# LayerNorm moved from the data into the weights of a float32 q/k projection, with deeper prefetch of x and of the mixing's rows

## The chip, the cores and the metric

The kernel runs on one core of one Trainium2 chip. A core has TensorE (PE in the profile, with its weight loads as PEld), VectorE (DVE), ScalarE (ACT), GpSimd (POOL) and SyncE (SP), which here issues every DMA. The engines run their own instruction lists in order and meet at semaphores. The metric is the device time of one execution in microseconds (us).

## The reference

Two gated residual steps on x of shape (8, 512, 2048), all float32. `_layernorm` normalises over the last axis (2048) without weights.

```python
x = x + tanh(g_xattn[0]) * xattn(_layernorm(x), ctx, mask, Wq, bq, Wk, bk, Wv, bv, Wo, bo)
x = x + tanh(g_ffn[0])   * ffn(_layernorm(x), W_res, W_pre, W_post, ...)

# xattn: patches of 128 along the last axis, 8 heads of 32
q = Wq @ qp + bq;  k = Wk @ qp + bk;  val = Wv @ vp + bv      # Wq, Wk, Wv: 256 x 512; qp from layernorm(x), vp from ctx
attn = softmax(where(mask, q^T k / sqrt(32), -1e9));  o = gelu(attn @ val)
out = (Wo @ o + bo) * mask

# ffn: 4 streams of 512 in each row of 2048
x_norm = x * rsqrt(mean(x*x) + eps)
H_res = sinkhorn_log(x_norm @ W_res.T + base, 50 iterations)   # 4 x 4 for each row
H_pre, H_post = softmax(x_norm @ W_pre.T + ..), softmax(x_norm @ W_post.T + ..)
y = (sum_n H_pre[n] * stream[n]) @ W_branch
out stream i = sum_j H_res[i, j] * stream[j] + H_post[i] * y
```

The normalised row d of x is (x[d] - mean[d]) * rstd[d]. In the projection d is the contracted index, so rstd[d] and mean[d] belong to the partition on which row d lies.

## The kernel before

The work is cut into 32 blocks (8 batches of 4), each 512 columns of x, with 4 steps of 128 columns. For block n, `load_x` brings four tiles of 128x512 into the pool `xp` (16 tiles). `proj(n)` makes q and k. For each of the four tiles, GpSimd writes the normalised xn (L500), ScalarE rounds it to a float16 xh (L505), GpSimd makes the float16 rest xl (L507). Then for each of four 128-row groups m of q and k TensorE adds twelve float16 matmuls in PSUM: WqkH on xh, WqkH on xl, WqkL on xh for each of four tiles (L518 to L520). ScalarE and VectorE evacuate the sum as a float16 pair ev (L522, L523), which goes to DRAM (qd) and comes back as QS and KS (`stack`, L535).

After that, for each step: `smax` (L569, L571), `expo` (L595, L597), `vproj` (L559, a float32 matmul), `attv` (L612 to L620); for each block `outp` (mask L632, gl L657, output projection L667 to L670, the sum into the x tile L671, and its store to x1s, L674). An x tile is taken at the load and given back after the store in `outp`, one block after its attention. `stats(b)` reads x and xT of the next batch for its mean, rstd and logits (`finish_stats` gives rstd and nb = -mean * rstd).

When a batch is through, `ffn` runs its Sinkhorn chain on VectorE (L840 to L863), and the rows are mixed: 20 groups of 128 rows by `mixv` (ScalarE, GpSimd and VectorE: xpre L920 to L925, y on TensorE L905 to L907, w L939 to L949), and 12 groups by `mixp` on TensorE, at the end of the program (L959 to L1004). `mixv` loads its four rows-tiles x1 from x1s as it starts (pool of 4) and writes through w (2 tiles).

The order is set by hand in the main loop, by the string ORDER and by priorities; the framework then places each engine's instructions by a modelled timeline, so a change of one operation can move others. `load_x` stands at letter "l":

```python
if LXP == 4 and p == 3 and n > 0 and n + 3 < NTOT:
    defer(D_LX, "lx", lambda n=n: load_x(n + 3))
```

D_LX and D_OUT are 0, so these are issued at once.

Of the kernel before, what the change touches and what calls it, by code (L numbers as in the profile page):

```python
# [19 lines left out]
P = 128  # L20
# [5 lines left out]
BLK = 512  # L26
NBLK = S // BLK
# [8 lines left out]
CT_ACT = False  # L36
MH_ACT = False
XS_ACT = False
LXP = 4
POOLMIX = lambda i, j: j == 1 and i > 0  # L40
BUF_GP = 1
BUF_OP = 1
BUF_XHP = 5
BUF_XNP = 2
BUF_XTP = 4
BUF_CTP = 2
BUF_QDP = 3
# [9 lines left out]
MIXL = 1  # L57
HALF = 1
ORDER = "MeoaMgPlsMMvSMpOM"
BUF_W = 2  # L60
BUF_X1 = 4
BUF_PJ = 1
BUF_PH = 1
BUF_EP = 2
BUF_XPRE = 1
PSTEPS = (0,1,1,2)
SP0 = 1
XH_POOL = lambda c: False
CAP = 1.0
NORM0 = True  # L70
D_MH = 0
# [1 line left out]
D_X1 = 0  # L73
D_OUT = 0
D_ST = 0
D_LX = 0
CT_PRE = False
BUF_XP = 16
PE_MIX = ((), (), (), (), (3,), (0, 1, 2, 3), (0, 1, 2, 3), (1, 2, 3))
SPLITS = (1, 1, 1, 1, 1, 1, 1, 1)  # L80
CHAINS = ((0,), (1,), (2,), (3,), (4,), (5,), (6,), (7,))
# [1 line left out]
PE_IN = ((), (), (), (), (), (), (), ())  # L83
# [16 lines left out]
def gated_xattn_mhc_kernel(  # L100
# [22 lines left out]
    B = x.shape[0]  # L123
    NTOT = B * NBLK
# [4 lines left out]
    def ctile(shape, dt, name):  # L129
        return const.tile(shape, dt, tag=name, name=name)  # L130
# [13 lines left out]
    onesb = ctile([P, P], F32, "onesb")  # L144
    V.memset(onesb, 1.0)

    WqkH = ctile([P, 4, 512], F16, "WqkH")
    WqkL = ctile([P, 4, 512], F16, "WqkL")
    Wv = ctile([P, 4, DK], F32, "Wv")
    WoH = ctile([P, 2, 512], F32R, "WoH")  # L150
    WoL = ctile([P, 2, 512], F32R, "WoL")
# [22 lines left out]
    mrow_d = dram.tile([6, B * S], BF16, tag="mrow_d", name="mrow_d")  # L174
    mneg_d = dram.tile([1, B * S], F16, tag="mneg_d", name="mneg_d")
    brow_d = dram.tile([3, 512], F32, tag="brow_d", name="brow_d")


    QS = [ctile([99, NH, SB], F16, f"QS{i}") for i in range(NS)]
# [6 lines left out]
    xnp = ctx.enter_context(tc.tile_pool(name="xnp", bufs=BUF_XNP))  # L186
# [32 lines left out]
    rawx = {}  # L219
    nmean = {}  # L220
    rstd1 = {}
    nb1 = {}
    sq2 = {}
    x1s = {}
    G4 = {}
# [24 lines left out]

    def finish_stats(b, nm, var):
        r = rsqrt(ln0, var, eps_ln, 4, "ln1")
        nb = ln0.tile([P, 4], F32, tag="nb1", name="nb1")
        V.tensor_tensor(nb, nm, r, ALU.mult)
        nmean[b], rstd1[b], nb1[b] = nm, r, nb

    with tc.tile_pool(name="set", bufs=1) as st:

# [66 lines left out]
        for t in range(2):  # L325
            sl = slice(256 * t, 256 * t + 256)
            V.tensor_scalar(wq[:, :, sl], wq[:, :, sl], al[:, t : t + 1], None, ALU.mult)
        A.copy(WqkH, wq)
        V.tensor_tensor(WqkL, wq, WqkH, ALU.subtract)
        for t in range(2):  # L330
            V.tensor_scalar(bqs[:, 2 * t : 2 * t + 2], bcol[:, 2 * t : 2 * t + 2], al[:, t : t + 1], None, ALU.mult)

# [10 lines left out]
        var0 = stile([P, 4], F32, "var0")  # L343
        V.tensor_copy(var0, mv[:, :, 1])
        finish_stats(0, nm, var0)


        mh = stile([B * 16, 3, P], BF16, "mh")
# [91 lines left out]
    def stats(b):  # L440

        lgs = xsp.tile([P, 512], F32, tag="lgs", name="lgs", bufs=1)
        for q4 in range(5):
            if q4 > 0:
                flush(lambda e: e[2] == "st")
                lg = ps_t.tile([P, 512], F32, tag="t", name="lgx")
                for g in range(4):
                    T.matmul(lg[32 * g : 32 * g + 32, :], Wm[:, 4 * q4 - 4 + g, :], xts[g], start=True, stop=True)  # L448
                if q4 == 1:
                    V.tensor_copy(lgs, lg)  # L450
                else:
                    V.tensor_tensor(lgs, lg, lgs, ALU.add)
            if q4 < 4:
                xts = []

                def ld(q4=q4, xts=xts):
                    for g in range(4):
                        xt_ = xtp.tile([P, 512], F32, tag="xTt", name="xTt")
                        k = 4 * q4 + g
                        SY.dma_start(xt_, xT[b, k * P : (k + 1) * P, :])  # L460
                        xts.append(xt_)

                defer(D_ST, "st", ld)
# [12 lines left out]
        sq = lnp.tile([P, 4, NBLK], F32, tag="sq1", name="sq1")  # L476
        for c in range(4):
            for k in range(NBLK):
                xs = xtp.tile([P, BLK], F32, tag="xTt", name="xs")
                (A if XS_ACT else SY).dma_start(xs, x[b, c * P : (c + 1) * P, k * BLK : (k + 1) * BLK])  # L480
                A.activation(xs, xs, AF.Square, bias=nm[:, c : c + 1], accum_out=sq[:, c, k : k + 1])
            if c % 2:
                yield 1
        var = lnp.tile([P, 4], F32, tag="var1", name="var1")
        V.tensor_reduce(var, sq, AX.X, ALU.add)
        V.tensor_scalar(var, var, 1.0 / S, None, ALU.mult)
        finish_stats(b, nm, var)
        yield 1

    qds = {}  # L490

    def proj(n):

        b, k = divmod(n, NBLK)
        flush(lambda e: e[2] == "lx")
        xt = xtile[n]
        hs, ls = [], []
        for c in range(4):
            xn = xnp.tile([P, BLK], F32, tag="xn", name="xn")
            G.tensor_scalar(xn, xt[c], rstd1[b][:, c : c + 1], nb1[b][:, c : c + 1], ALU.mult, ALU.add)  # L500
            h = xhp.tile([P, BLK], F16, tag="xh", name="xh")
            if XH_POOL(c):
                G.tensor_copy(h, xn)
            else:
                A.copy(h, xn)  # L505
            l = xhp.tile([P, BLK], F16, tag="xl", name="xl")
            G.tensor_tensor(l, xn, h, ALU.subtract)  # L507
            hs.append(h)
            ls.append(l)
        if NORM0:  # L510
            yield
        qd = qdp.tile([2, 4, 2, P, BLK], F16, tag="qd", name="qd")
        qds[n] = qd
        for m in range(4):
            ps = ps_p.tile([P, BLK], F32, tag="p", name="qk")
            ms = slice(m * P, (m + 1) * P)
            for c in range(4):
                T.matmul(ps, WqkH[:, c, ms], hs[c], start=(c == 0), stop=False)  # L518
                T.matmul(ps, WqkH[:, c, ms], ls[c], start=False, stop=False)  # L519
                T.matmul(ps, WqkL[:, c, ms], hs[c], start=False, stop=(c == 3))  # L520
            ev = evp.tile([P, 2, BLK], F16, tag="ev", name="ev")
            A.activation(ev[:, 0, :], ps, AF.Identity, bias=bqs[:, m : m + 1])  # L522
            V.scalar_tensor_tensor(ev[:, 1, :], ps, bqs[:, m : m + 1], ev[:, 0, :], ALU.add, ALU.subtract)  # L523
            defer(D_QD, "qd", lambda m=m, ev=ev: SY.dma_start(qd[m // 2, 0:2, m % 2].rearrange("t p s -> p t s"), ev))
            yield

    def stack(m):
# [362 lines left out]

    def mix(b, maps):
        E, cst, pre, prc, post, rec, HR = maps
        for c in range(4):
            if c in PE_IN[b - B]:
                yield from mixp(b, c, maps, True)
            elif c not in PE_MIX[b - B]:
                yield from mixv(b, c, maps)

    def branch(pt, ph, pl, y):

# [8 lines left out]
    def mixv(b, n, maps):  # L909

        E, cst, pre, prc, post, rec, HR = maps
        x1 = []
        for j in range(4):
            t = fp.tile([P, 512], F32, tag="x1", name="x1", bufs=BUF_X1)
            SY.dma_start(t, x1s[b][n * P : (n + 1) * P, 512 * j : 512 * j + 512])
            x1.append(t)
# [20 lines left out]
        for i in range(4):  # L937
# [12 lines left out]
            defer(D_OUT if live[0] else 0, "out", lambda i=i, w=w: SY.dma_start(out[b, n * P : (n + 1) * P, 512 * i : 512 * i + 512], w))  # L950
            yield 1

    def mixp(b, n, maps, inp=False):
# [56 lines left out]
    def run(gen, steps=None):  # L1010
        for _ in gen:
            pass

    run(proj(0))
    stack(0)
    vproj(0)
    for t in range(2):
# [29 lines left out]
    def act(c, t):  # L1047
# [18 lines left out]
            if p == 2:  # L1066
                at("stack", stack, NSB * (n + 1) + 1)
        elif c == "l" and live_:
            if LXP == 4 and p == 3 and n > 0 and n + 3 < NTOT:
                defer(D_LX, "lx", lambda n=n: load_x(n + 3))  # L1070
            if LXP == 5 and p == 2 and n > 0 and n + 3 < NTOT:
                defer(D_LX, "lx", lambda n=n: load_x(n + 3))
            if p == LXP and n > 1 and n + 2 < NTOT:
                defer(D_LX, "lx", lambda n=n: load_x(n + 2))
# [121 lines left out]
```

## Time and profile before

| | |
|---|---|
| median of 3 runs | 1835.11 us (1830.48 to 1844.21) |
| the profiled execution | 1828.05 us, span 1825.9 us |
| TensorE busy | 1547.1 us (85%) |
| VectorE busy | 1382.3 us (76%) |
| ScalarE busy | 1069.4 us (59%) |
| GpSimd busy | 602.8 us (33%) |
| mean granted TensorE clock | 0.932 |
| DMA | 330.60 MB, mean 181 GB/s |

The profile is of one execution. Busy time is the union of an engine's instructions; "L518" is line 518 of the kernel before. A group line gives engine, operation, output and inputs, shape and count, then busy time, mean time of one, and the idle time ahead of it with what ended it. A wait line reads: engine and line, what it waited for, then total us, number of waits, longest. Matmuls are pipelined, so their own durations overlap, and the distance between two starts tells what one costs. Each float32 matmul appears as two instructions.

### The profile page before, as it was taken

To read this page: it belongs to the slowest core of one execution; us is meant where nothing else is said; L and a number is where in the kernel's file an instruction comes from. 1 tells how busy PE (TensorE), PEld (TensorE's weight loads), DVE (VectorE), ACT (ScalarE), POOL (GpSimd) and SP (SyncE) were. 2 spreads that over 40 slices of the span, in tenths; PEclk is the share of its full clock that TensorE was granted. 3 is DMA by queue.
4 is the path that set the end of the run, shared out by engine and by line. 5 is a ranking of instruction groups with operands and counts; after the bars stand their busy time and mean duration, and the time that the engine had idled before them with its cause. 6 is when DMAs were issued, how large, how long until landed. Compare 5 with 4: busy or idle time off the path is not lost.

```text
span 1825.9 us, 32268 instructions
## 1 busy us (share of the span) xinstructions
PE 1547.1 (85%) x10517; PEld 901.0 (49%) x10517; DVE 1382.3 (76%) x4201; ACT 1069.4 (59%) x2030; POOL 602.8 (33%) x511
## 2 busy tenths in 40 slices
PE   3998999989889888889878888799888889768887
PEld 2554555555555554545544445455455555543333
DVE  7434345877888778888888879889898998998761
ACT  2386466646555656558565475566665566755454
POOL 0512222322232243342444333444334442321121
PEclk7999999999999988999988999899999999989999
DMA  6478696467646855568555784468755565523443
GB/s 214 139 209 256 208 258 194 140 174 232 180 134 200 254 169 165 151 192 269 162 154 164 214 251 144 139 196 259 215 154 165 148 189 147 172 93 119 144 157 117
DMA packets 353237, 330.60 MB, mean 181 GB/s; under 512 B 53351, under 2 KB 251303, under 8 KB 353070
## 3 DMA queue, kind: packets, MB, share of 16 engines
q1 hardware_dynamic: 353070, 328.55, 60.6%
q8 instruction: 83, 1.36, 0.3%
q14 instruction: 84, 0.69, 0.1%
HBM read 226.71 MB, written 101.16 MB: 180 GB/s over the span
## 4 chain that ended last, share of the span: by engine, by line
PE 37%; DVE 23%; DMA 18%; issue 9%; ACT 9%; POOL 4%; SPq 1%; ACTq 0%; POOLq 0%; DVEq 0%
PE vp L559 5%; DVE w L946 4%; DMA xs<-in_x_dram 4%; PE qk L518 3%; PE qk L519 3%; DMA out_dram<-w 3%; PE qk L520 3%; DMA x<-x1s 2%; PE mx L1000 2%; DMA x1s<-xt 2%; PE lgx L448 2%; DVE mx L571 2%; PE op L667 2%; DVE W L844 2%; PE mx L1001 2%
## 5 line engine op out<-in xcount | busy, mean ns | idle before, releaser
L559 PE MATMUL vp<-Wv,ct 128*128 128x256 f32 x1024 | 272.4, 418 | 16.7 <-DMA ct<-in_cx_dram 15.1
L500 POOL TENSOR_SCALAR xn<-xt,ln_r,nb 128x512 f32<-128x512 f32 x128 | 105.5, 826 | 501.2 <-DMA xt<-in_x_dram 385.7
L559 PEld LDWEIGHTS vp<-Wv,ct 128*128 128x128 f32 x1024 | 207.4, 210 | 68.0 <-issue 18.6
L518 PE MATMUL qk<-xh,WqkH 128*128 128x512 f16 x512 | 199.2, 390 | 29.4 <-ACT xh L505 16.3
L946 DVE SCALAR_TENSOR_TENSOR w<-x,Et,w 128x512 f32<-128x512 f32 x180 | 180.0, 1001 | 49.6 <-POOL w L944 34.0
L519 PE MATMUL qk<-xl,WqkH 128*128 128x512 f16 x512 | 197.9, 387 | 4.3 <-POOL xl L507 4.0
L520 PE MATMUL qk<-xh,WqkL 128*128 128x512 f16 x512 | 197.6, 386 | 0.0
L571 DVE TENSOR_REDUCE mx<-smax 128x8 f32<-128x1024 f32 x128 | 154.9, 1210 | 41.7 <-PE smax L569 41.3
L507 POOL TENSOR_TENSOR xl<-xn,xh 128x512 f16<-128x512 f32 x128 | 156.3, 1228 | 76.0 <-ACT xh L505 70.4
L597 ACT ACTIVATE e<-sT,ebi,esc 128x1024 f32<-128x1024 f32 x128 | 153.4, 1198 | 18.0 <-PE sT L595 17.9
L523 DVE SCALAR_TENSOR_TENSOR ev<-qk,bqs,ev 128x512 f16<-128x512 f32 x128 | 94.5, 739 | 77.5 <-ACT ev L522 76.1
L667 PE MATMUL op<-gh,WoH 128*128 128x512 f32 x256 | 120.9, 474 | 35.3 <-DVE ev L523 31.1
L944 POOL TENSOR_TENSOR w<-w,pj 128x512 f32<-128x512 f32 x60 | 80.1, 1334 | 213.1 <-ACT w L939 113.7
L505 ACT CAST xh<-xn 128x512 f16<-128x512 f32 x128 | 78.3, 612 | 103.7 <-POOL xn L500 102.9
L522 ACT ACTIVATE ev<-qk,bqs 128x512 f16<-128x512 f32 x128 | 86.9, 679 | 85.0 <-PE qk L520 78.7
L673 ACT ACTIVATE junk<-xt,nmean 128x512 bf16<-128x512 f32 x128 | 91.6, 716 | 73.9 <-DVE xt L671 41.3
L850 DVE TENSOR_TENSOR W<-E,uv 128x64 f32<-128x64 f32 x392 | 119.4, 307 | 5.4
L844 DVE TENSOR_TENSOR W<-E,uv 128x64 f32<-128x64 f32 x352 | 117.1, 335 | 4.8
L612 PE MATMUL u<-e,onesb 128*32 128x256 f32 x1024 | 102.7, 403 | 10.5 <-DVE mq L573 3.8
L668 PE MATMUL op<-gl,WoH 128*128 128x512 f32 x256 | 107.1, 418 | 0.0
L669 PE MATMUL op<-gh,WoL 128*128 128x512 f32 x256 | 106.6, 417 | 0.0
L632 POOL TENSOR_TENSOR o<-o,mb 128x1024 f32<-128x1024 f32 x32 | 75.6, 2364 | 93.2 <-ACT o L627 85.9
(287 smaller groups left out, 3504.6 us busy)
## 6 DMA issues: line engine op xcount, KB each, us to landing
xt<-in_x_dram SPq DMA_DIRECT2D x128, 256.0 KB
ct<-in_cx_dram SPq DMA_DIRECT2D x128, 256.0 KB
xTt<-in_xT_dram SPq DMA_DIRECT2D x128, 256.0 KB
qd<-ev SPq DMA_DIRECT2D x128, 256.0 KB
x1s<-xt SPq DMA_DIRECT2D x128, 256.0 KB
xs<-in_x_dram SPq DMA_DIRECT2D x112, 256.0 KB
QS<-qd SPq DMA_DIRECT2D x192, 128.0 KB
KS<-qd SPq DMA_DIRECT2D x192, 128.0 KB
```

Source lines behind the costliest of these rows:

```text
L507: G.tensor_tensor(l, xn, h, ALU.subtract)
L518: T.matmul(ps, WqkH[:, c, ms], hs[c], start=(c == 0), stop=False)
L519: T.matmul(ps, WqkH[:, c, ms], ls[c], start=False, stop=False)
L520: T.matmul(ps, WqkL[:, c, ms], hs[c], start=False, stop=(c == 3))
L559: T.matmul(ps[:, h, :], ct[:, c, :], Wv[:, c, :], start=(c == 0), stop=(c == 3))
L571: V.tensor_reduce(mx, sc, AX.X, ALU.max)
L597: A.activation(e32, sc, AF.Exp, bias=ebi[:, t : t + 1], scale=esc[:, t : t + 1])
L667: T.matmul(ps, WoH[:, e, cs], gh[:, e], start=(e == 0), stop=False)
L668: T.matmul(ps, WoH[:, e, cs], gl[:, e], start=False, stop=False)
L844: V.tensor_tensor(W4[:, h], E4[:, h], vb[:, h], ALU.mult)
L850: V.tensor_tensor(W4[:, h], E4[:, h], ub[:, h], ALU.mult)
L946: V.scalar_tensor_tensor(w, x1[j], E[:, n, 4 * j + i : 4 * j + i + 1], w, ALU.mult, ALU.add)
```

## The change

The projections of q and k no longer read a normalised copy of x. With w = W * rstd per contracted row, W @ ((x - mean) * rstd) = w @ x - w @ mean. So `weights(b, m)` makes, for each batch b and group m, a float32 tile of scaled weights (GpSimd, four instructions of 128x128), multiplies it with the negated mean on TensorE (four matmuls with one column), and VectorE adds the bias. The scaled Wq and Wk are kept in DRAM (wqk_d) and loaded anew for each batch after the first. `proj` then has four float32 matmuls per group on the x tiles themselves; xn, xh, xl, WqkH and WqkL are gone. For the next batch, groups 0 and 1 are prepared at the end of `stats`, groups 2 and 3 in the last block of the batch that is running, into a pool of 6 tiles.

The x pool has 20 tiles, and `load_x` runs four blocks ahead. In `mix`, the four x1 tiles of the next 128 rows are loaded after the second of four output tiles of the present ones (`fetch`, 8 tiles), and w has 3 tiles. The pool of xh and xl, now used by `mixp` alone for the halves of its branch, has 1 tile of each (5 before).

```diff
-LXP = 4
-BUF_XHP = 5
-BUF_XNP = 2
+BUF_XHP = 1
+BUF_WQ = 6
-BUF_W = 2
-BUF_X1 = 4
+BUF_W = 3
+BUF_X1 = 8
-BUF_XP = 16
+BUF_XP = 20
...
+    def weights(b, m, src=None):
+        w = wqp.tile([P, 4, P], F32, tag="wq", name="wqb")
+        if src is None:
+            SY.dma_start(w, wqk_d[m])
+            src = w
+        for c in range(4):
+            G.tensor_scalar(w[:, c], src[:, c], rstd1[b][:, c : c + 1], None, ALU.mult)
+        bp = ps_t.tile([P, BLK], F32, tag="t", name="bp")[:, 0:1]
+        for c in range(4):
+            T.matmul(bp, w[:, c], nmean[b][:, c : c + 1], start=(c == 0), stop=(c == 3))
+        bi = ln0.tile([P, 1], F32, tag=f"bi{m}", name="bi")
+        V.tensor_tensor(bi, bp, bqs[:, m : m + 1], ALU.add)
+        wqb[b, m] = (w, bi)
...
-        A.copy(WqkH, wq)
-        V.tensor_tensor(WqkL, wq, WqkH, ALU.subtract)
+        for m in range(4):
+            SY.dma_start(wqk_d[m], wq[:, :, m * P : (m + 1) * P])
...
+        for m in range(4):
+            weights(0, m, wq[:, :, m * P : (m + 1) * P])
...
         finish_stats(b, nm, var)
+        for m in range(2):
+            weights(b, m)
...
-        for c in range(4):
-            xn = xnp.tile([P, BLK], F32, tag="xn", name="xn")
-            G.tensor_scalar(xn, xt[c], rstd1[b][:, c : c + 1], nb1[b][:, c : c + 1], ALU.mult, ALU.add)
-            h = xhp.tile([P, BLK], F16, tag="xh", name="xh")
...
-            l = xhp.tile([P, BLK], F16, tag="xl", name="xl")
-            G.tensor_tensor(l, xn, h, ALU.subtract)
...
+            if (b, m) not in wqb:
+                weights(b, m)
+            w, bi = wqb[b, m]
             for c in range(4):
-                T.matmul(ps, WqkH[:, c, ms], hs[c], start=(c == 0), stop=False)
-                T.matmul(ps, WqkH[:, c, ms], ls[c], start=False, stop=False)
-                T.matmul(ps, WqkL[:, c, ms], hs[c], start=False, stop=(c == 3))
+                T.matmul(ps, w[:, c], xt[c], start=(c == 0), stop=(c == 3))
...
+            if k == NBLK - 1 and m < 2 and (b + 1, 1) in wqb:
+                weights(b + 1, m + 2)
...
+        own = [c for c in range(4) if c not in PE_IN[b - B] and c not in PE_MIX[b - B]]
+        ahead = {}
+
+        def fetch(c):
+            if c in ahead or c not in own:
+                return
+            ahead[c] = []
+            for j in range(4):
+                t = fp.tile([P, 512], F32, tag="x1", name="x1", bufs=BUF_X1)
+                SY.dma_start(t, x1s[b][c * P : (c + 1) * P, 512 * j : 512 * j + 512])
+                ahead[c].append(t)
...
+            elif c in own:
+                fetch(c)
+                yield from mixv(b, c, maps, ahead[c], lambda c=c: fetch(c + 1))
...
+            if i == 1:
+                after_first()
...
     run(proj(0))
+    load_x(NBLK)
...
-            if LXP == 4 and p == 3 and n > 0 and n + 3 < NTOT:
-                defer(D_LX, "lx", lambda n=n: load_x(n + 3))
...
+            if p == 3 and n > 0 and n + 4 < NTOT:
+                load_x(n + 4)
```

More of the change, by code (lines that the diff above doesn't have):

```diff
@@ L67 @@
 SP0 = 1
-XH_POOL = lambda c: False
 CAP = 1.0
@@ L75 @@
 D_ST = 0
-D_LX = 0
 CT_PRE = False
-BUF_XP = 16
+BUF_XP = 20
 PE_MIX = ((), (), (), (), (3,), (0, 1, 2, 3), (0, 1, 2, 3), (1, 2, 3))
@@ L145, in gated_xattn_mhc_kernel @@
     V.memset(onesb, 1.0)
-    WqkH = ctile([P, 4, 512], F16, "WqkH")
-    WqkL = ctile([P, 4, 512], F16, "WqkL")
     Wv = ctile([P, 4, DK], F32, "Wv")
@@ L176, in gated_xattn_mhc_kernel @@
     brow_d = dram.tile([3, 512], F32, tag="brow_d", name="brow_d")
+    wqk_d = dram.tile([4, P, 4, P], F32, tag="wqk_d", name="wqk_d")
     QS = [ctile([99, NH, SB], F16, f"QS{i}") for i in range(NS)]
@@ L185, in gated_xattn_mhc_kernel @@
     xsp = ctx.enter_context(tc.tile_pool(name="xsp", bufs=2))
-    xnp = ctx.enter_context(tc.tile_pool(name="xnp", bufs=BUF_XNP))
+    wqp = ctx.enter_context(tc.tile_pool(name="wqp", bufs=BUF_WQ))
     xhp = ctx.enter_context(tc.tile_pool(name="xhp", bufs=BUF_XHP))
@@ L221, in gated_xattn_mhc_kernel @@
     rstd1 = {}
-    nb1 = {}
+    wqb = {}
     sq2 = {}
@@ L252, in finish_stats @@
         r = rsqrt(ln0, var, eps_ln, 4, "ln1")
-        nb = ln0.tile([P, 4], F32, tag="nb1", name="nb1")
-        V.tensor_tensor(nb, nm, r, ALU.mult)
-        nmean[b], rstd1[b], nb1[b] = nm, r, nb
+        nmean[b], rstd1[b] = nm, r
+    def weights(b, m, src=None):
[11 more added lines that the diff above has]
+        wqb[b, m] = (w, bi)
     with tc.tile_pool(name="set", bufs=1) as st:
@@ L494, in proj @@
         b, k = divmod(n, NBLK)
-        flush(lambda e: e[2] == "lx")
         xt = xtile[n]
-        hs, ls = [], []
-        for c in range(4):
-            xn = xnp.tile([P, BLK], F32, tag="xn", name="xn")
-            G.tensor_scalar(xn, xt[c], rstd1[b][:, c : c + 1], nb1[b][:, c : c + 1], ALU.mult, ALU.add)
-            h = xhp.tile([P, BLK], F16, tag="xh", name="xh")
[L502 to L505, printed above, removed]
-            l = xhp.tile([P, BLK], F16, tag="xl", name="xl")
-            G.tensor_tensor(l, xn, h, ALU.subtract)
-            hs.append(h)
-            ls.append(l)
         if NORM0:
@@ L515, in proj @@
             ps = ps_p.tile([P, BLK], F32, tag="p", name="qk")
-            ms = slice(m * P, (m + 1) * P)
+            if (b, m) not in wqb:
+                weights(b, m)
+            w, bi = wqb[b, m]
             for c in range(4):
-                T.matmul(ps, WqkH[:, c, ms], hs[c], start=(c == 0), stop=False)
-                T.matmul(ps, WqkH[:, c, ms], ls[c], start=False, stop=False)
-                T.matmul(ps, WqkL[:, c, ms], hs[c], start=False, stop=(c == 3))
+                T.matmul(ps, w[:, c], xt[c], start=(c == 0), stop=(c == 3))
             ev = evp.tile([P, 2, BLK], F16, tag="ev", name="ev")
-            A.activation(ev[:, 0, :], ps, AF.Identity, bias=bqs[:, m : m + 1])
-            V.scalar_tensor_tensor(ev[:, 1, :], ps, bqs[:, m : m + 1], ev[:, 0, :], ALU.add, ALU.subtract)
+            A.activation(ev[:, 0, :], ps, AF.Identity, bias=bi)
+            V.scalar_tensor_tensor(ev[:, 1, :], ps, bi, ev[:, 0, :], ALU.add, ALU.subtract)
             defer(D_QD, "qd", lambda m=m, ev=ev: SY.dma_start(qd[m // 2, 0:2, m % 2].rearrange("t p s -> p t s"), ev))
+            if k == NBLK - 1 and m < 2 and (b + 1, 1) in wqb:
+                weights(b + 1, m + 2)
             yield
@@ L895, in mix @@
                 yield from mixp(b, c, maps, True)
-            elif c not in PE_MIX[b - B]:
-                yield from mixv(b, c, maps)
+            elif c in own:
+                fetch(c)
+                yield from mixv(b, c, maps, ahead[c], lambda c=c: fetch(c + 1))
     def branch(pt, ph, pl, y):
@@ L907, in branch, with mixv @@
             T.matmul(y, pl[:, e, :], WbH[:, e, :], start=False, stop=(e == 3))
-    def mixv(b, n, maps):
+    def mixv(b, n, maps, x1, after_first):
         E, cst, pre, prc, post, rec, HR = maps
[L912 to L916, printed above, removed]
         for _ in range(MIXL):
@@ L949, in mixv @@
             V.scalar_tensor_tensor(w, y, post[:, n, i : i + 1], w, ALU.mult, ALU.add)
-            defer(D_OUT if live[0] else 0, "out", lambda i=i, w=w: SY.dma_start(out[b, n * P : (n + 1) * P, 512 * i : 512 * i + 512], w))
+            SY.dma_start(out[b, n * P : (n + 1) * P, 512 * i : 512 * i + 512], w)
+            if i == 1:
+                after_first()
             yield 1
@@ L1068, in act @@
         elif c == "l" and live_:
-            if LXP == 4 and p == 3 and n > 0 and n + 3 < NTOT:
-                defer(D_LX, "lx", lambda n=n: load_x(n + 3))
[L1071 to L1074, printed above, removed]
+            if p == 3 and n > 0 and n + 4 < NTOT:
+                load_x(n + 4)
         elif c == "s" and live_ and t + AHEAD < NT_:
```

## The prediction

> **What bounds the kernel now.** I first cut the span into four stages (busy time per engine in given stretches; the columns are length, then busy us and instruction count of PE, PEld, DVE, ACT, POOL, then granted clock, DMA share, GB/s).
>
> ```profile
> 0.00:60.00 60.00, 24.57 (x76) 14.14 (x77) 40.67 (x93) 16.68 (x22) 14.92 (x19) 0.72 0.55 174
> 60.00:600.00 540.00, 497.11 (x3739) 298.08 (x3738) 335.04 (x948) 318.92 (x618) 157.31 (x139) 0.97 0.68 199
> 600.00:1560.00 960.00, 807.73 (x5735) 491.83 (x5733) 818.46 (x2359) 594.84 (x1143) 378.45 (x306) 0.92 0.63 186
> 1560.00:1826.00 266.00, 217.67 (x970) 96.97 (x970) 188.16 (x803) 138.92 (x249) 52.16 (x48) 0.95 0.40 131
> ```
>
> The reader is to see two regimes. From 60 to 600 us (attention, no mixing yet) TensorE is busy 92% at clock 0.97 and VectorE 62%: TensorE bounds. From 600 to 1560 us, with the mixing, both stand at 84 to 85% and the clock is 0.92: no engine is full, they wait for each other. The last 266 us hold no projection (the next view shows x0). The same query for line 518 alone, the first of the three f16 matmuls, says where the change acts:
>
> ```profile
> 60.00:600.00 540.00, 81.25 (x214) 20.73 (x213) 0.97 0.68 199
> 600.00:1560.00 960.00, 112.74 (x288) 28.48 (x288) 0.92 0.63 186
> 1560.00:1826.00 266.00, 0.00 (x0) 0.00 (x0) 0.95 0.40 131
> ```
>
> Next, TensorE's timeline, since mean durations overlap: the starts count.
>
> ```profile
> 76.50 0.38 PE L518 MATMUL qk<-xh,WqkH 128*128 128x512 f16 x1
> 76.72 0.38 PE L519 MATMUL qk<-xl,WqkH 128*128 128x512 f16 x1
> 76.94 0.38 PE L520 MATMUL qk<-xh,WqkL 128*128 128x512 f16 x1
> ...
> 1751.59 1.02 PE L1000 MATMUL mx<-ys,QD 128*128 128x512 f32 x2
> 1752.45 1.02 PE L1001 MATMUL mx<-xc,HD 128*128 128x512 f32 x2
> ```
>
> One f16 matmul of 512 columns takes 0.216 us from start to start, one float32 matmul of that size (two instructions) 0.86 us. Last, the waits from 600 to 1560 us:
>
> ```profile
> POOL xn L500 <- DMA xt<-in_x_dram: 191.0, 54, 15.8
> ACT w L939 <- DMA out_dram<-w: 42.4, 31, 5.4
> ACT pj L924 <- DMA x<-x1s: 37.5, 24, 3.9
> PE op L667 <- DVE ev L523: 26.0, 18, 4.9
> ACT xpre L920 <- DMA x<-x1s: 18.9, 15, 3.9
> ```
>
> ScalarE stands for 98.8 us behind the mixing's transfers; POOL's 191 us are spare time, since TensorE waited for xh and xl only some 20 us in the whole span.
>
> **The projections.** Three f16 matmuls (0.648 us) become one float32 matmul (0.86 us): +0.212 us for each of 512. By the view of L518: 214 x 0.212 = 45 us in the early stage, 288 x 0.212 = 61 us in the middle, 2 us before.
>
> **The bias products.** 32 groups of four float32 matmuls with one column. The nearest row is rawp L467 (128x32, float32), whose instructions follow each other every 112 ns, two to a matmul: 0.22 us each, 0.9 us a group, 28 us in all. Four groups fall in setup, about 9 us in the early stage, 16 us in the middle. Ends: 0.14 us each, as L420 (128x1) ran (18 us), or 0.44, as L406 ran at half clock (56 us).
> They can also wait: 28 groups need a fresh weight tile. The SP queue issues its load once the old tile is released, POOL scales it, then TensorE may go. Behind a bias product stands all of TensorE's queue, first of all the output projection and the next q/k columns; behind the load, every transfer, as all are issued by SP. In the changed order 12 of the 28 groups have only 78 to 160 entries of TensorE's list (some 240 a block, so a third to two thirds of a block, 15 us or more) between the release and the product; for the others it is over 370 or nothing is released. A 256 KB load has taken 4 to 5 us in the chain of waits, the four scalings 1 us. Ends: 0, and 12 x 5 = 60 us if no distance is left; I take 5 us, because of the distance.
>
> **What goes from POOL, ScalarE and VectorE.** POOL loses xn (105.5 us) and xl (156.3 us), ScalarE the cast (78.3 us). POOL gains 128 scalings of 128x128: L500 takes 826 ns for four times as much, so from 207 ns each up to 826; I take 250, 32 us. VectorE's 32 bias additions (129 ns, as kap L323) are 4 us, against 3 us for the old nb. POOL sets no end here, but it slows VectorE. Read instruction by instruction, w L946 (two SBUF inputs) takes 740 ns (median of 81) where no POOL instruction overlaps it, and 1218 ns (mean of 99) where one does; the reduction L571 takes 1215 ns either way. Adding such excesses by the overlapping POOL line gives 54.7 us for L507 (74 cases) and 8.2 us for L500 (26), some 50 of them after 600 us. The Trainium skill, "SBUF — State Buffer", section "Who interferes with whom", says that a VectorE instruction with two SBUF inputs and a POOL instruction reading SBUF exclude each other for a whole instruction. By that rule each pair costs half of the POOL instruction: 74 x 0.61 + 26 x 0.41 = 56 us, and the new scalings take back some 6. I use the row, 63 - 6 = 57 us. VectorE's middle stage falls from 818 to about 768 us.
>
> **The transfers.** x four blocks ahead and 20 tiles: POOL's wait is no longer a step, but matmuls read x directly, so a late x would hold TensorE; a whole block of lead (40 to 55 us) against a 4 to 5 us load hides it. x<-x1s ahead (8 tiles) takes away 37.5 + 18.9 us of ScalarE's stalls, the third w tile most of 42.4. What is late next is TensorE's own queue. The weights add 32 transfers of 256 KB, 8 MB on 330: hidden at a DMA share of 0.63. The single xh/xl buffer in the tail costs nothing: the next y there starts only after the mixing matmuls, 7 us, in which the cast (0.58 us) fits.
>
> **Setup.** rstd now waits on VectorE behind wo L381, 10.0 us for its DMA; in the changed order it stands ahead. But wo then stands ahead of the first evacuation, and wo's load moves from the 41st to the 63rd place on SP: 22 issues of 0.64 us, 14 us later, about 50 us against the first evacuation at 54.5 us now. From -10 to +8; I take -3.
>
> **Clock.** Granted: 0.97 where TensorE is 92% busy, 0.92 where 84%. The Trainium skill, "TensorE: Matmul & The Clock Gate", Part 1, says that the clock is either half or full, by the activity in windows of 3.4 us. The changed middle would have 808 + 61 + 16 = 885 us of matmul in 960, 92%, like the early stage. By the row alone (clock stays 0.92) it needs 885 / 0.92 = 962 us: no change. By the rule, if the clock rises to 0.97 as in the early stage, 885 x 0.92 / 0.97 = 839 us, at 92% busy 912 us: -48.
>
> **Sum.** Early stage: 45 + 9 = 54 us of new matmul against 43 us of idle, of which few waits are the removed ones; I let 9 be absorbed: +45. Middle: between -48 and +2, with the added waits; I take -15, near the row, because VectorE stays at 80% and both must fit. Bias waits +5, setup -3, tail 0. In all +32 on the profiled execution's own 1828.05 us (span 1825.9 and 2.2 around it): 1860. The median of the runs, 1835.11, lies 0.4% above that execution, so I give 1863, 1.5% above the median. A measurement of this kernel tells about 1% from no change.
>
> **Rivals.**
> *The stalls were the bound (faster).* If ScalarE's 98.8 us and POOL's interference set the middle, it shrinks until TensorE is full: 885 at clock 0.97 is 839 us; at 95% busy 883, -77. With +30 early: about 1780. For it: x<-x1s, out<-w and L946 are 4.7, 5.1 and 7.0% of the middle's chain. Against: the early stage is bound by the engine that gets the work.
> *They cancel (within 1%).* Early +45, middle -48: 1828 to 1835. For it: the chain's qk share is 17% early but only 5% in the middle.
> *TensorE passes everything on (slower).* Idle stays as it is: 54 + 77 us, 1960 at most; with half of the middle, 1920. For it: TensorE's waits in the middle have many owners, the largest, op<-ev, only 26 us.
> *The weights hold TensorE (slower).* 12 stalls of 5 us at the bias products instead of 5 us in all: 1860 + 55 = 1915. It decides from about 2 us a stall on. For it: POOL works in order, and w L944 there has waited up to 20.9 us for ScalarE. Against: the 15 us of distance.
> That the change doesn't do what it says is excluded by the order: qk is one float32 matmul, POOL's list is without xn and xl.
>
> **Numbers.** Forecast 40%, cancel 25%, stalls 25%, passed on 6%, weights 4%. The forecast's own range, from the middle's ends and the bias and setup bounds, is 1830 to 1890. Outside 1775 to 1915 I leave about 2 in 10. Faster by over 1%: 0.28 (the stalls and a little of cancel); within 1%: 0.25; slower: 0.47.
>
> **What would show it.** Early stage (to the point where the mixing starts) about 45 us longer, TensorE at 94% or more there; qk at 0.86 us from start to start; clock of the middle 0.94 to 0.97; L946's mean near 900 ns; ACT<-x1s waits below 15 us; the tail as long as before. It is wrong if the early stage grows by under 25 us, if the middle shrinks by over 50 us, or if bias products show waits on POOL of over 30 us.

## The result, and the profile after

The changed kernel takes 1901.53 us (median of 4 runs, 1897.97 to 1904.26) against 1833.38 us (4 runs) for the kernel before: 1.0359 times as long (95% interval 1.0313 to 1.0406). That is 68 us more; the forecast was 32 more. The profiled execution took 1897.97 us, span 1896.2.

To compare stages I cut both spans at the same work, not at the same times: at the first exp of block 0, of block 12 (nearly all of the mixing comes after it), and of block 31 (the last).

| stage | before, us | after, us | forecast | measured |
|---|---|---|---|---|
| setup, to block 0 | 85.1 | 88.5 | -3 | +3.4 |
| early, blocks 0 to 11 | 510.2 | 564.8 | +45 | +54.6 |
| middle, blocks 12 to 30 | 995.2 | 1009.0 | -15 | +13.8 |
| tail | 235.4 | 233.9 | 0 | -1.5 |

Busy time of the engines in these stretches, first for the kernel before (columns: stretch and its length, busy us and instruction count of PE, PEld, DVE, ACT, POOL, then granted clock, DMA share, GB/s):

```profile
85.00:595.00 510.00, 467.11 (x3566) 280.86 (x3564) 321.85 (x920) 304.85 (x594) 140.30 (x122) 0.97 0.68 199
595.00:1590.00 995.00, 837.26 (x5978) 510.74 (x5970) 848.69 (x2469) 618.19 (x1187) 390.23 (x314) 0.92 0.63 185
```

and for the changed kernel:

```profile
88.00:653.00 565.00, 513.77 (x3467) 306.81 (x3486) 329.58 (x966) 285.22 (x558) 87.95 (x86) 0.97 0.66 189
653.00:1662.00 1009.00, 890.47 (x5777) 546.25 (x5819) 846.34 (x2494) 578.21 (x1109) 284.31 (x235) 0.94 0.63 184
1662.00:1896.00 234.00, 190.30 (x757) 78.40 (x757) 162.24 (x656) 117.66 (x210) 39.48 (x39) 0.96 0.37 125
```

Early, TensorE is busy 47 us longer and idle 8 us longer (510 - 467 = 43 before, 565 - 514 = 51 after): none of the idle time took up new work. In the middle TensorE is busy 53 us longer and its idle time falls only from 158 to 119 us. POOL lost a quarter of its work there, ScalarE 40 us; VectorE lost nothing (848.7 before, 846.3 after).

The same view of the new projection line alone (columns: PE, PEld, clock, DMA share, GB/s) tells where the new matmuls lie:

```profile
88.00:653.00 565.00, 181.23 (x384) 70.53 (x384) 0.97 0.66 189
653.00:1662.00 1009.00, 274.34 (x576) 107.85 (x576) 0.94 0.63 184
```

At two instructions each these are 192 and 288 float32 matmuls. Their price is read from the starts of their weight loads in the timeline (start, duration, engine, line and operation):

```profile
126.19 0.19 PEld L521 LDWEIGHTS qk<-xt,wqb 128*128 128x128 f32 x1 [0.24 <-issue]
126.62 0.19 PEld L521 LDWEIGHTS qk<-xt,wqb 128*128 128x128 f32 x1 [0.24 <-issue]
127.05 0.19 PEld L521 LDWEIGHTS qk<-xt,wqb 128*128 128x128 f32 x1 [0.24 <-issue]
```

One every 0.43 us, so 0.86 us a matmul, as forecast. The kernel before had 185 threes of float16 matmuls between the same two points early and 292 in the middle, by L518:

```profile
85.00:595.00 510.00, 70.40 (x185) 17.93 (x185) 0.97 0.68 199
595.00:1590.00 995.00, 114.27 (x292) 28.87 (x292) 0.92 0.63 185
```

So the early stage has 192 x 0.86 - 185 x 0.648 = 45 us more projection, and 12 groups of bias products at 0.9 us make it 56; in the middle it is 58 and 14, about 73 together.

Next the costliest groups of the changed kernel, the projections and VectorE's mixing (busy time, mean ns of one, idle time before with its main cause):

```profile
L521 PE MATMUL qk<-xt,wqb 128*128 128x512 f32 x1024 | 490.9, 619 | 21.2 <-DVE ev L524 15.0
L957 DVE SCALAR_TENSOR_TENSOR w<-x,Et,w 128x512 f32<-128x512 f32 x180 | 160.1, 899 | 32.5 <-POOL w L955 25.4
```

The mixing's instruction (L946 before, 1001 ns) is down to 899 ns, the value forecast for it. That is 20 us less VectorE time, yet the engine's busy time rose from 1382.3 to 1384.3 us.

Last, waits of the changed kernel, from 653 to 1662 us (engine and line, what it waited for, total us, times, longest):

```profile
ACT w L950 <- DMA out_dram<-w: 61.8, 33, 4.8
PE vp L562 <- DMA ct<-in_cx_dram: 14.9, 6, 4.6
PE op L670 <- DVE ev L524: 14.1, 10, 2.7
PE bp L262 <- POOL wqb L259: 0.6, 3, 0.2
```

The waits of ScalarE for x<-x1s in the mixing (37.5 and 18.9 us) are gone. But the one for the output tiles, 42.4 us before, is now 61.8, although w has a third tile. Why is not shown: the kernel before with the same new mixing (e4 below) has 36.0 us of it. TensorE's waits have no large owner, and the bias products wait on POOL 0.6 us here, 4.0 us in the whole span.

### The profile page after: what moved, and what is told of

It is laid out like the page before. It is cut to its first block, busy times and chain, and to the rows that moved or that the text cites. A ratio compares the mean times of both kernels' runs of the same rounds, so it can differ in the third digit from the quotient of the medians.

```text
span 1896.2 us, 31495 instructions
## 1 busy us (share of the span) xinstructions
PE 1651.2 (87%) x10195; PEld 963.9 (51%) x10261; DVE 1384.3 (73%) x4224; ACT 998.2 (53%) x1901; POOL 421.9 (22%) x383
## 5 line engine op out<-in xcount | busy, mean ns | idle before, releaser
L521 PE MATMUL qk<-xt,wqb 128*128 128x512 f32 x1024 | 490.9, 619 | 21.2 <-DVE ev L524 15.0
L521 PEld LDWEIGHTS qk<-xt,wqb 128*128 128x128 f32 x1024 | 191.0, 196 | 219.6 <-issue 185.6
L957 DVE SCALAR_TENSOR_TENSOR w<-x,Et,w 128x512 f32<-128x512 f32 x180 | 160.1, 899 | 32.5 <-POOL w L955 25.4
L523 ACT ACTIVATE ev<-qk,bi 128x512 f16<-128x512 f32 x128 | 86.9, 679 | 179.6 <-PE qk L521 170.8
L635 POOL TENSOR_TENSOR o<-o,mb 128x1024 f32<-128x1024 f32 x32 | 75.4, 2356 | 416.0 <-ACT o L630 345.6
L524 DVE SCALAR_TENSOR_TENSOR ev<-qk,bi,ev 128x512 f16<-128x512 f32 x128 | 94.8, 741 | 86.2 <-ACT ev L523 82.4
L493 ACT ACTIVATE xs<-xs,nmean 128x512 f32<-128x512 f32 x112 | 79.9, 714 | 64.1 <-DMA xs<-in_x_dram 46.9
L674 DVE TENSOR_TENSOR xt<-op,xt 128x512 f32<-128x512 f32 x128 | 87.0, 680 | 32.6 <-PE op L673 17.3
L950 ACT ACTIVATE w<-x,sm,Et 128x512 f32<-128x512 f32 x80 | 63.9, 809 | 83.0 <-DMA out_dram<-w 62.3
L855 DVE TENSOR_REDUCE sm<-W 128x16 f32<-128x64 f32 x392 | 101.5, 260 | 8.0
L621 ACT ACTIVATE rc<-u 128x256 f32<-128x256 f32 x128 | 47.7, 373 | 108.8 <-PE u L619 77.2
L572 PE MATMUL smax<-KS,QS 97*128 97x128 f16 x1024 | 83.9, 223 | 22.8 <-ACT mh L581 16.9
```

Of the source, the lines that this page charges most:

```text
L521: T.matmul(ps, w[:, c], xt[c], start=(c == 0), stop=(c == 3))
L524: V.scalar_tensor_tensor(ev[:, 1, :], ps, bi, ev[:, 0, :], ALU.add, ALU.subtract)
L855: V.tensor_reduce(sm[:, h], W4[:, h].rearrange("p n i j -> p n j i"), AX.X, ALU.add)
L957: V.scalar_tensor_tensor(w, x1[j], E[:, n, 4 * j + i : 4 * j + i + 1], w, ALU.mult, ALU.add)
```

## The experiments

My theory after the result: TensorE's new work (108 us of float32, 28 us of bias products) is passed on almost whole, in the middle too, and what POOL, ScalarE and the prefetch give back is worth far less than the 92 us that the forecast set against it there. Rivals: the change's own new waits (the bias products' PSUM tile, the x tiles) cost the difference; the new mixing does harm; or the rearranged instruction lists do, since the framework plans all engines' lists anew at every edit.

Each ratio is to executions of the kernel before that ran beside the run, with medians of 1833 to 1838 us. Stage lengths are of one profiled execution each, cut as above.

| run | median us | ratio to before (95%) | setup / early / middle / tail, us |
|---|---|---|---|
| before | 1833.38 | 1 | 85.1 / 510.2 / 995.2 / 235.4 |
| after | 1901.53 | 1.0359 (1.0313 to 1.0406) | 88.5 / 564.8 / 1009.0 / 233.9 |
| e1: before + a 4th float16 matmul | 1949.23 | 1.0645 (1.0602 to 1.0687) | 87.1 / 579.4 / 1045.7 / 232.1 |
| e2: after, 3 of 4 row tiles | 1846.94 | 1.0072 (1.0045 to 1.0100) | 90.8 / 525.9 / 993.6 / 232.6 |
| e3: after, old mixing | 1934.49 | 1.0544 (1.0515 to 1.0574) | 89.6 / 557.8 / 1039.5 / 240.2 |
| e4: before, new mixing | 1859.49 | 1.0126 (1.0068 to 1.0183) | 84.8 / 527.4 / 1018.0 / 231.9 |
| e5: before, 2 of 3 float16 matmuls | 1827.40 | 0.9944 (0.9926 to 0.9963) | 89.2 / 497.0 / 1005.0 / 236.4 |
| e6: after, no bias products | 1859.35 | 1.0125 (1.0100 to 1.0151) | 88.1 / 542.6 / 994.2 / 232.2 |
| e7: e2 and e6 together | 1797.16 | 0.9782 (0.9750 to 0.9813) | 88.5 / 517.5 / 954.0 / 234.9 |
| e8: before, 17 x tiles | 1846.70 | 1.0085 (1.0053 to 1.0116) | 79.8 / 516.9 / 1008.3 / 235.1 |
| e9: after, x as before | 1917.62 | 1.0444 (1.0408 to 1.0481) | 84.8 / 561.2 / 1030.3 / 238.9 |
| e10: after, bias in another PSUM pool | 1948.64 | 1.0609 (1.0570 to 1.0648) | 100.2 / 567.4 / 1040.5 / 232.9 |
| e11: after, 21 x tiles | 1902.22 | 1.0340 (1.0276 to 1.0404) | 95.6 / 556.1 / 1017.2 / 235.3 |
| e12: after, reduced float32 | 1800.32 | 0.9805 (0.9737 to 0.9873) | 80.7 / 508.0 / 970.5 / 234.7 |
| e13: e7, old mixing | 1839.04 | 1.0023 (1.0008 to 1.0039) | 90.0 / 499.2 / 1011.0 / 238.9 |
| e14: e13, old x loads | 1808.26 | 0.9864 (0.9833 to 0.9895) | 83.5 / 493.4 / 990.5 / 238.0 |
| e15: after, bias products doubled | 1924.29 | 1.0500 (1.0428 to 1.0573) | 99.2 / 560.9 / 1021.6 / 228.4 |

### How much of TensorE's work reaches the end

**e2: a quarter of the float32 projection left out (108 us of TensorE).** The last row tile is not added.

```diff
-            for c in range(4):
-                T.matmul(ps, w[:, c], xt[c], start=(c == 0), stop=(c == 3))
+            for c in range(3):
+                T.matmul(ps, w[:, c], xt[c], start=(c == 0), stop=(c == 2))
```

> The changed kernel with three of the four row tiles in the q/k products (the fourth 128 rows of x are left out of q and k): 3 x 0.86 = 2.58 us a group, what the twelve f16 matmuls took. Only TensorE's added projection time is taken out. Theory A: the early stage falls back by about 45 us and the middle falls below the kernel before, since POOL and ScalarE stay relieved: 1790 to 1830 us. Theory B: it stays above 1870 us.

Measured: 55 us less than the changed kernel, half of what was taken away, between the two forecasts: 39 us early, where 44 us of matmul went, and only 15 in the middle, where 62 went.

**e6: the bias products left out (28 us of TensorE).** The bias is made from nmean directly, so the loads, scalings and the addition stay.

```diff
-        bp = ps_t.tile([P, BLK], F32, tag="t", name="bp")[:, 0:1]
-        for c in range(4):
-            T.matmul(bp, w[:, c], nmean[b][:, c : c + 1], start=(c == 0), stop=(c == 3))
-        V.tensor_tensor(bi, bp, bqs[:, m : m + 1], ALU.add)
+        V.tensor_tensor(bi, nmean[b][:, m : m + 1], bqs[:, m : m + 1], ALU.add)
```

> The changed kernel with the 128 one-column matmuls taken out (the mean's part of the bias is left out, the bias addition stays, reading the mean itself). They are 0.22 us each by their starts in the profile after, 28 us. If they cost their time on TensorE alone: 1870 to 1880 us. If their waits hold TensorE's list: under 1860. If they are hidden: 1895 to 1905.

Measured: 42 us less, more than the 28 us of matmul that went. The surplus lies early (22 us less for about 11 of matmul); the middle is 15 us shorter for 14.

**e7: both edits of e2 and e6.** The projection then costs 3 x 0.86 = 2.58 us a group, as the twelve float16 matmuls did (12 x 0.216 = 2.59): TensorE's work is that of the kernel before, the rest is that of the changed kernel.

> The changed kernel with both parts of TensorE's added time taken out (three of four row tiles in the q/k products, no one-column matmuls; both leave terms of q and k out). TensorE's work is that of the kernel before; POOL and ScalarE stay relieved, x and the mixing's rows are loaded ahead. Theory A with a gain from the rest (1901 - 108 - 28 = 1765, if all passes): 1760 to 1800 us. Theory C (TensorE's time given back only in part, the three-tile run gave 55 of 108): 1820 to 1835 us, no gain over the kernel before.

Measured: 104 us less than the changed kernel, 41 us (2.2%) less than the kernel before. Its busy times:

```profile
88.00:606.00 518.00, 468.82 (x3291) 280.84 (x3289) 316.75 (x933) 283.08 (x554) 89.29 (x86) 0.96 0.72 205
606.00:1560.00 954.00, 805.97 (x5529) 500.95 (x5529) 826.24 (x2499) 579.31 (x1113) 282.34 (x234) 0.94 0.67 194
```

Against the kernel before the early stage is 7 us longer and the middle 41 us shorter (954 for 995). So in this kernel, at equal TensorE work, everything else in the change is worth 41 us, all of it in the middle; the added 136 us of TensorE (some 54 early, 76 in the middle) then cost 47 us early and 55 in the middle. That gives the result: -41 + 55 = +14 in the middle, +7 + 47 = +54 early. How far the -41 depends on the order of the lists is seen in e13 and e14.

**e1: the kernel before with 110 us of TensorE work added.** A fourth float16 product.

```diff
-                T.matmul(ps, WqkL[:, c, ms], hs[c], start=False, stop=(c == 3))
+                T.matmul(ps, WqkL[:, c, ms], hs[c], start=False, stop=False)
+                T.matmul(ps, WqkL[:, c, ms], ls[c], start=False, stop=(c == 3))
```

> The kernel before with a fourth f16 matmul (WqkL on xl) for each tile: four of 0.216 us in the place of three, so TensorE gets the 0.216 x 512 = 110 us that float32 costs more, while POOL, ScalarE, VectorE and all transfers keep what they had. Theory A (the added TensorE time passes on, fully where TensorE bounds, partly in the middle, and the rest of the change gives a little back): early stage +45 us, middle +30 to +60, in all 1905 to 1940 us. Theory B (TensorE's time is mostly hidden, the loss of the change comes from its other parts, the weights and the new order): under 1865 us.

Measured: 115 us more for 110 us of matmul, above both forecasts. By stage it is not so even: 69 us early, where some 44 us were added, and 50 in the middle, where some 60 were.

```profile
87.00:667.00 580.00, 522.58 (x3770) 302.94 (x3791) 339.26 (x965) 307.50 (x601) 143.64 (x126) 0.97 0.61 178
667.00:1712.00 1045.00, 891.59 (x6219) 540.93 (x6249) 878.46 (x2493) 617.97 (x1178) 388.10 (x312) 0.92 0.60 175
```

In the middle TensorE is busy 54 us longer and is idle 153 us, as before (158); VectorE's busy share stays at 84%. A middle in which TensorE is busy only 84 to 85% still passes on most of what is added to it. The 25 us early beyond the added work have no cause that the run shows.

**e5: the kernel before with 110 us of TensorE work taken away.**

```diff
-                T.matmul(ps, WqkH[:, c, ms], ls[c], start=False, stop=False)
-                T.matmul(ps, WqkL[:, c, ms], hs[c], start=False, stop=(c == 3))
+                T.matmul(ps, WqkH[:, c, ms], ls[c], start=False, stop=(c == 3))
```

> The kernel before without the third f16 matmul (WqkL on xh is left out of q and k): TensorE loses 0.216 x 512 = 110 us, all else keeps its work. A fourth matmul cost 115 us. Theory A (the time follows TensorE's list whole, in both directions, its idle share staying): 1715 to 1745 us. Theory C (TensorE passes on what is added, since it becomes the bound, but what is taken away is not given back, as other engines bound the middle): 1775 to 1800 us.

Measured: 11 us less, a smaller gain than in either forecast.

```profile
89.00:586.00 497.00, 436.77 (x3349) 264.24 (x3346) 306.31 (x876) 299.88 (x587) 139.32 (x121) 0.93 0.70 201
586.00:1591.00 1005.00, 807.93 (x5701) 505.66 (x5694) 858.14 (x2494) 621.97 (x1195) 387.94 (x314) 0.87 0.62 184
```

The granted clock fell from 0.97 to 0.93 early and from 0.92 to 0.87 in the middle, so that TensorE's busy time fell by only 30 and 29 us where 43 and 61 of matmul had gone. The middle did not shorten at all; VectorE is busy 85% of it. The kernel before thus stands at a bend: more TensorE work is paid nearly in full, less brings almost nothing.

**e15: the bias products doubled (28 us of TensorE added to the changed kernel).** Nothing else is added: no tile, no wait.

```diff
-        for c in range(4):
-            T.matmul(bp, w[:, c], nmean[b][:, c : c + 1], start=(c == 0), stop=(c == 3))
+        for j in range(8):
+            c = j % 4
+            T.matmul(bp, w[:, c], nmean[b][:, c : c + 1], start=(j == 0), stop=(j == 7))
```

> The changed kernel with each bias product run twice into the same PSUM column (eight matmuls in the place of four; the mean's part of the bias is doubled): 28 us more matmul, no further tile, wait or load. If the matmuls' time is all: 1925 to 1935 us. If the surplus of 14 us lies in slots, waits and loads that come once: no more than that. If one-column matmuls cost more than their starts show: above 1940 us.

Measured: 23 us more, just below the first forecast; its four runs spread from 1912 to 1940 us. That agrees with the matmul time passing on, and with the other 14 us of e6's 42 not being the matmuls' own time, but the stages do not show it cleanly (setup 11 us longer, early 4 shorter, middle 13 longer, tail 6 shorter). The runs do not tell whether the 14 us come from the PSUM tile, from a wait, or from another plan of the lists.

### Whether new waits take the difference

**e10: the bias products' sum in the projections' PSUM pool.**

```diff
-        bp = ps_t.tile([P, BLK], F32, tag="t", name="bp")[:, 0:1]
+        bp = ps_p.tile([P, BLK], F32, tag="p", name="bp")[:, 0:1]
```

> The changed kernel with the bias products in the PSUM pool of the projections (tag p) in the place of the pool of transposes and attention sums (tag t); the same matmuls. Taking the products out gave 42 us for 28 us of matmuls. If the surplus comes from the two buffers of the pool t that they occupy: 1880 to 1892 us. Rival, from the new order of the lists or the weight loads alone: 1893 to 1915 us.

Measured: 47 us more, a miss on all sides. Setup grew by 12 us and the middle by 31. Perhaps the projections' pool is the scarcer one; the run does not show it, and does not tell what the original place costs.

**e9: x loaded as before, 16 tiles and three blocks ahead.**

```diff
-BUF_XP = 20
+BUF_XP = 16
...
-    load_x(NBLK)
...
-            if p == 3 and n > 0 and n + 4 < NTOT:
-                load_x(n + 4)
+            if p == 3 and n > 0 and n + 3 < NTOT:
+                load_x(n + 3)
```

> The changed kernel with x as before: 16 tiles, loaded three blocks ahead. If the deeper load of x carries part of the gain at equal TensorE work (float32 matmuls read x directly, so a late x holds TensorE's list): 1915 to 1940 us, with waits of qk for xt in the profile. Rival, x is hidden anyway and only the order of the lists changes: 1885 to 1918 us.

Measured: 16 us more than the changed kernel. In the middle, TensorE now waits for x; the changed kernel has no such wait there:

```profile
PE qk L521 <- DMA xt<-in_x_dram: 38.0, 20, 5.3
```

So the longer lead is no source of loss, and it takes away a wait of TensorE itself. The 16 us alone would prove little: e8 below moves the time by 9 us without such a reason.

**e11: 21 x tiles (`BUF_XP = 21`).**

> The changed kernel with 21 x tiles in the place of 20, nothing else: the same instructions in newly planned lists. The same edit on the kernel before moved the time by 0.8%. If a new plan alone is worth that here too: within 1890 to 1917 us, and this is the bound for reading any one edit. If it is worth more: outside that.

Measured: 1902.22 us, no difference; its runs spread from 1882.8 to 1906.3. The x tiles are not short.

**e3: the changed kernel with the old mixing** (rows loaded as each group starts, 4 and 2 tiles).

```diff
-BUF_W = 3
-BUF_X1 = 8
+BUF_W = 2
+BUF_X1 = 4
...
-            if i == 1:
-                after_first()
```

> The changed kernel with the mixing of before: no load ahead, 4 x1 tiles, 2 w tiles. If the prefetch gave what the prediction's sum let it give in the middle (half of ScalarE's 98.8 us of stalls), 1925 to 1950 us. Rival: with TensorE near full the prefetch is worth nothing, 1890 to 1910 us.

Measured: 33 us more, 30 of them in the middle and 6 in the tail, the early stage 7 less. With the old mixing ScalarE's waits for x<-x1s are back in the middle (39.1 and 38.2 us). In the changed kernel the new mixing is a gain.

### What the relief is worth, and what a new plan costs

**e4: the kernel before with the new mixing alone** (`fetch`, 8 and 3 tiles, as in the change).

> The kernel before with the changed mixing alone (next rows loaded ahead, 8 x1 tiles, 3 w tiles), f16 projections and x as before. If ScalarE's stalls behind the mixing's transfers set the middle: 1785 to 1815 us. Rival, another wait takes their place at once: 1825 to 1845 us.

Measured: 25 us more, where I and the rival had seen a gain or nothing. The early stage grew by 17 us and the middle by 23, although ScalarE's waits for x<-x1s are gone from the middle and out<-w fell from 42.4 to 36.0 us. Set side by side, the lists of VectorE, ScalarE and GpSimd first differ in block 5, at about 300 us. That is also where the first four loads of rows ahead are issued (286 to 295 us), so the run does not part a new plan of the lists from the transfers.

**e8: the kernel before with one more x tile (`BUF_XP = 17`).** It adds a buffer and not one instruction.

> The kernel before with 17 x tiles in the place of 16 and nothing else. No instruction is added or taken away; but the lists of all engines are planned anew, and differ in order over most of the program. If the order alone is worth little: 1830 to 1840 us. If each new plan moves the time by itself: anything from 1800 to 1870 us, beyond 1% from the kernel before.

Measured: 0.85% more (0.53 to 1.16), 9 us; setup 5 us shorter, early 7 and middle 13 longer. Since a spare buffer alone gives no reason for a longer middle, I take some 10 us as what a new plan of the lists can be worth; that reading is argued, not shown, and nothing bounds it from above.

**e13: e7 with the old mixing. e14: e13 with the old x loads.** In e14 TensorE has the work of the kernel before, the transfers are as before but for the 32 loads of weights, and only POOL's, ScalarE's and VectorE's relief is left. The edits are those of e3 and e9.

> e7 (three of four row tiles in the q/k products, no bias products: TensorE works as much as before) with the mixing of before. If the mixing's load ahead makes most of the 41 us by which e7 beats the kernel before: 1822 to 1840 us (33 us more than e7, as in the changed kernel). If POOL's and ScalarE's lost work makes most of it: 1797 to 1812 us.

> e13 with x in 16 tiles, three blocks ahead, too. What then parts it from the kernel before is only the lost work of POOL (xn, xl, against 81 us of weight scaling) and ScalarE (the cast), and the weight loads, at equal TensorE work. If that lost work is worth nothing: 1832 to 1855 us, at or above the kernel before. If it is worth the 50 us that VectorE lost to POOL in the prediction's sum: under 1800 us.

Measured: e13 is 42 us above e7 and level with the kernel before; e14 is 31 us below e13 and between its two forecasts, although it takes a prefetch away. With e14, the relief alone is 27 us below the kernel before (1.4%, 1.0 to 1.7):

```profile
84.00:577.00 493.00, 457.43 (x3250) 275.43 (x3272) 314.97 (x934) 281.75 (x551) 87.68 (x85) 0.98 0.72 211
577.00:1567.00 990.00, 838.87 (x5518) 515.28 (x5555) 829.86 (x2497) 578.09 (x1109) 283.19 (x234) 0.91 0.65 190
```

Of these 27 us only 5 lie in the middle, where the forecast had put nearly all of the relief; 17 are early. At one and the same TensorE work the middle takes 954 (e7), 990 (e14) and 1011 us (e13), against 995 before. So the 41 us that e7 gives back there are not the relief of the engines alone, and its two prefetches together with this order of the lists are part of it. The single prefetches have no fixed worth: the mixing's was 33 and 42 us in favour (e3, e13) and 25 against (e4), the x loads' 16 in favour (e9) and 31 against (e14).

### A version that beats both kernels

**e12: the changed kernel with reduced float32 projections** (x rounded by ScalarE to F32R, one instruction a matmul; x loads as in e9). Its q and k are made from rounded weights and a rounded x.

```diff
-        w = wqp.tile([P, 4, P], F32, tag="wq", name="wqb")
+        wr = wqp.tile([P, 4, P], F32R, tag="wq", name="wqb")
+        w = wr.bitcast(F32)
...
-        xt = xtile[n]
+        xt = []
+        for c in range(4):
+            xr = xhp.tile([P, BLK], F32R, tag="xr", name="xr", bufs=BUF_XR)
+            A.copy(xr, xtile[n][c])
+            xt.append(xr)
```

> The changed kernel with q and k from one reduced-float32 matmul (weights and a copy of x that ScalarE rounds, 128 x 0.61 us; x in 16 tiles, three blocks ahead). The output projection's matmuls of that kind start every 0.23 us, so TensorE loses 512 x (0.86 - 0.23) = 323 us against the changed kernel and stands 187 us below the kernel before. Theory C (TensorE's time is given back only down to where VectorE and the waits bound the middle; the three tiles without bias products, at the TensorE work of before, took 1797): 1740 to 1790 us. Theory A (TensorE's time follows whole): under 1680 us.

Measured: 1800.32 us, above both forecasts, 2.0% below the kernel before (1.3 to 2.6) and 101 us below the changed kernel, for 512 x (0.86 - 0.23) = 323 us of TensorE taken away. The projections' group and the busy times:

```profile
L527 PE MATMUL qk<-xr,wqb 128*128 128x512 f32 x512 | 193.1, 478 | 62.1 <-ACT xr L515 49.0 <-DVE ev L530 7.7 <-ACT VF L569 4.9
```

```profile
81.00:589.00 508.00, 427.78 (x3275) 285.63 (x3299) 300.65 (x887) 305.65 (x596) 88.82 (x87) 0.89 0.72 210
589.00:1559.00 970.00, 767.99 (x5466) 519.85 (x5499) 817.59 (x2442) 613.58 (x1180) 279.11 (x234) 0.85 0.66 192
```

TensorE is busy 84% early and 79% in the middle at a clock of 0.89 and 0.85, and it now waits 49 us for the rounding. VectorE stands at 84% of the middle (85% before). It has 187 us less TensorE work than e7 and is no faster, though the two also differ in the x loads and in the rounding: below the bend TensorE's work counts for little.

## Why the prediction was right or wrong

**Direction and early stage: right.** The term was 45 + 9 of new matmul less 9 absorbed. By the same work it was 56 us of matmul and +54.6 us of time. The absorption failed: idle time rose from 43 to 51 us. The sign "TensorE at 94% or more" failed with it, since 514 / 565 is 91%. The price of the float32 matmul (0.86 us) and of a bias product (its instructions follow each other every 111 to 112 ns, two to a matmul, 0.22 us) were as forecast. "No mixing yet" before 600 us was a little too strong: the first of the 20 groups is loaded from 161 us on and begins its sums at 320 us.

**Middle: the step that failed.** The sum took +77 of new matmul and -92 for all that would be given back, and came to -15; it was +14. By e7 everything given back is 41 us, not 92, and the new matmuls cost 55 us, not 77. What failed is the assumption under both ends of the range: the row (+2) and the rule of the Trainium skill, "TensorE: Matmul & The Clock Gate", Part 1 (-48), were each worked out with TensorE busy 92% of the middle, as in the early stage. It reached 890 / 1009 = 88%; in the kernel before, in e1 and in e7 it stood at 84 to 85% (837 / 995, 892 / 1045, 806 / 954). The clock did rise, from 0.92 to 0.94, which agrees with busy time growing by 53 us where 73 of matmul were added. But TensorE was idle 119 us, and a middle 15 us shorter than before (980 us) with the same 890 us of TensorE would have left room for 90. That idle time belongs to many small waits (the largest of TensorE's is 14.9 us), and the relief of the other engines took away only part of them. Why these waits last is open.

**VectorE's relief: a term that was met in part and bought less.** Its mixing instruction has the forecast mean, 899 ns, so the reading by overlap with POOL was right in size: added instruction by instruction from the trace, the time that VectorE loses to POOL fell from about 180 to 135 us, 45 less where 57 had been taken. The durations of all VectorE instructions together fell by 39 us, from 1608 to 1569, 28 of them in the middle. But busy time is their union, and it did not fall (1382.3 to 1384.3 us): successive records overlapped by 226 us before and by 185 after. So the forecast's step from a sum of shorter instructions to 50 us less busy time in the middle did not hold there. At the TensorE work of before it held in part: VectorE's busy time is 1349.3 us in e7 and 1355.7 in e14, and e14 as a whole is 27 us below the kernel before, not 57.

**ScalarE's waits: more than half are left.** x<-x1s is gone, as forecast (below 15 us), but out<-w, of which most was to go, grew by 19 us. Of 98.8 us of waits 62 are left.

**Waits of the bias products: right, and the price for them low.** 4.0 us on POOL against +5 forecast, the "weights hold TensorE" rival (12 stalls of 5 us) fell. Yet taking the products out gave 42 us for 28 of matmul; doubling them (e15) cost 23. What makes up the rest is open.

**Setup and tail: right within 7 us.** +3.4 and -1.5, forecast -3 and 0.

**Rivals.** "TensorE passes everything on" was nearest in mechanism: with half of the middle it gave 1920, at 6% of the chances. The runs show it nearly whole for work added to the kernel before (e1), and at 104 of 136 us for the change's own (e7 to after). The 1915 of "the weights hold TensorE" is nearer by number, but its stalls are not there. "The stalls were the bound" and "they cancel" fell in the middle by their own test, since it did not shrink.

**What stays open.** The worth of each single prefetch: e3, e4, e9, e13 and e14 give both signs, and an edit that adds no instruction already moves the time by some 10 us (e8). With that, the split of the middle into -41 and +55 is known to some tens of us only; that TensorE's work is what slows the changed kernel does not hang on it (e1, e2, e6, e7, e12). Whether the plan or the transfers make e4 slower is open. The scalings on POOL were mispriced too, at no visible cost:

```profile
L259 POOL TENSOR_SCALAR wqb<-wqb,ln_r 128x128 f32<-128x128 f32 x112 | 69.1, 635 | 118.6 <-DVE ln_r L244 65.4 <-DMA wqb<-wqk_d 34.7 <-PE smax L579 18.6
L259 POOL TENSOR_SCALAR wqb<-wq,ln_r 128x128 f32<-128x128 f32 x16 | 9.3, 602 | 25.4 <-DVE ln_r L244 25.4
```

They are 78 us in all, not the 32 of the sum (250 ns each).

## What to carry to other kernels

When a change trades cheap work on several engines for more work on one, first ask on which side of the bend that one stands: add and take away the same amount of its work (e1, e5), since the same engine here passed on 115 us for 110 added and gave back 11 of 110 taken. Relief of engines that do not end a stage is worth a fraction of their busy time (27 us in e14, 41 with the prefetches, for some 180 us less of POOL and 70 of ScalarE), and a removed wait need not shorten the kernel (e4). Where a framework plans the instruction lists, run an edit that changes as little as possible but the plan; differences of its size between single edits can't be put down to the edits.

## What the runs showed of the hardware

- The granted clock is lower where TensorE is less busy: mean over the span 0.948 at 87% busy in the changed kernel, 0.932 at 85% before, 0.894 at 81% in e5, 0.870 at 80% in e12. The traces hold only full and half clock, in stretches of whole multiples of 3.41 us: half for 249 us of the span before, for 200 us after. The lower clock took back part of what was saved, some 12 of 43 us early in e5 by busy time. The clock rows of the two pages, in tenths of full speed over 40 slices of the span, first of the changed kernel, then of e12:

```profile
PEclk8999999999999999999889998999999998889999
```

```profile
PEclk7797899898889988788689896998878889989999
```

  7 of the 40 slices stand below 9 in the first, 24 in the second.
- A POOL scaling of 128x128 took 602 to 635 ns, one of 128x512 826 ns: a quarter of the data in three quarters of the time.
- The new POOL scalings hardly disturb VectorE: by overlap its instructions lost 1.4 us to all 128 of them, where the larger two-input operations of POOL (gl L660 and o L635) cost 43 and 32 us. The mixing's two-input w L957 took 760 ns where only a scaling overlapped it (10 cases) and 741 ns where nothing of POOL did.
